# A decoder layer in fp32: the norms of the second queries and keys move from GpSimd to TensorE

## The chip, the cores and the metric

The kernel runs on one core of a Trainium2 chip. The metric is the device time of one launch in microseconds, the median of three runs. Profiles are of one execution taken by the hardware profiler; TensorE is called PE there, its weight loads PEld, VectorE DVE, ScalarE ACT, GpSimd POOL, and SyncE, which issues nearly all DMAs, SP.

## What is computed

A decoder layer on x (8 x 100 tokens of 1024) and a context (8 x 722 of 1024): a retention layer, an attention layer over context and own tokens, a gated feed-forward layer, each followed by a residual sum and a layer norm. The part that matters here stands at the start of the attention layer: queries (16 heads of 128) and keys (4 heads) are projected, each head is divided by the root of its mean square, and then turned by position (rope).

```python
def rms_norm(x, w, eps=EPS):
    var = jnp.mean(jnp.square(x), axis=-1, keepdims=True)
    return x * jax.lax.rsqrt(var + eps) * w
...
q = (x @ wq).reshape(B, L, NUM_HEADS, HEAD_DIM)
k = (x @ wk).reshape(B, L, NUM_KV_HEADS, HEAD_DIM)
v = (x @ wv).reshape(B, L, NUM_KV_HEADS, HEAD_DIM)
q = rms_norm(q, q_norm_w)
k = rms_norm(k, k_norm_w)
...
q = q * cos + rotate_half(q) * sin
k = k * cos + rotate_half(k) * sin
```

## The kernel before

Everything is fp32 in effect. An operand of a large matmul is split into a high and a low part in the reduced fp32 type (`split`, `split2`, lines 64 to 70: ScalarE casts the high part, VectorE subtracts for the low part), and `mm3` (lines 87 to 90) makes three passes of TensorE for one product. Small matmuls (sums over partitions, transposes, the first layer's scores) are plain fp32.

Features lie on partitions and tokens on the free axis. The 800 tokens are worked in two halves of N = 400 (4 sequences of 100). A "block" below is one projection of one head for one half: 128 features x 400 tokens, 24 passes (`proj`, lines 102 to 107), left in a PSUM bank. There are eight banks: three of tag a, four of tag s, one of tag v; projections take a and s in turn (`acc_tag`).

The stage in question is the loop at lines 608 to 640. For each of the four groups of heads it projects four queries, a key and a value (i = 0 to 3, 4, 5) in chunks of two weight matrices, or four in the first chunk, each chunk for both halves. Weights come in by SP (`load_w`, line 72, three raw buffers wst), and are split into one of four buffers w. A query or key block then goes through these steps:

1. line 631, ScalarE: squares sq out of the bank;
2. line 632, `all_red` (line 127), GpSimd: sum of the squares over the 128 partitions, on every partition;
3. line 634, `rope` (lines 135 to 139): two half copies on ScalarE, three products and sums on VectorE; the bank is free after line 137;
4. line 635, `inv_root` (lines 115 to 122): Ln, Exp, Square on ScalarE, two operations on VectorE, all on 128 x 400;
5. line 636, VectorE: the turned block times scale and root;
6. lines 639 and 640: split into d, one DMA to the DRAM tensor qd or kd.

A value block is transposed on TensorE (`tokens_first`, line 150) and written to vd. Into the same stage the context keys of the first two groups of heads are worked ahead (`context_keys`, lines 578 to 596), with four more GpSimd reductions at line 591 and weights from the DRAM tensor wcd (line 84). The loop over sequences from line 647 reads qd, kd and vd back. There, at lines 595 and 674, a row of sums already goes through DRAM to come back as a column.

The order of the instructions on each engine is not that of the text. The program is planned by a simulated timeline: at each step the planner gives an engine the earliest instruction of the text that is ready by its own estimates. On the chip each engine then runs its list in order and waits at semaphores, so a wait that is longer than planned holds all that stands behind it on that engine, DMA issues on SP included. Tiles of one tag share the buffers given by bufs, and a new tile waits for the last reader of the one before.

Of the kernel before, what the change touches and what calls it, by code (L numbers as in the profile page):

```python
# [8 lines left out]
F32 = mybir.dt.float32  # L9
FR = mybir.dt.float32r  # L10
AF = mybir.ActivationFunctionType
ALU = mybir.AluOpType
# [4 lines left out]
P = 128  # L17
B, T, D = 8, 100, 1024
NB = 4
N = NB * T  # L20
# [11 lines left out]
NKV = 4  # L32
# [9 lines left out]
def decoder_layer(ctx, tc, xT, cT, w1, wo1, w2, wo2, wc, w3, wd, gw, qw, kw, trig, dec, mask, out):  # L42
    nc = tc.nc

    def sbuf(name, bufs, side=None):
        return tc.tile_pool(name=name, bufs=bufs, side=side, reuse_waits="tile")
# [3 lines left out]
    dr = ctx.enter_context(tc.tile_pool(name="dr", bufs=1, space=DRAM))  # L50
# [4 lines left out]
    def bank(tag):  # L55
        return ps.tile([P, 512], F32, tag=tag, name=tag, bufs=banks[tag])

    def f32(ap):
        return ap.bitcast(F32)

    def bt(ap):
        return ap.rearrange("p (b t) -> p b t", b=NB)
# [5 lines left out]
    def split2(hi, lo, src):  # L68
        nc.scalar.copy(hi, src)  # L69
        nc.vector.tensor_tensor(lo, src, f32(hi), ALU.subtract)  # L70

    def load_w(src, w=None, parts=1):
        st = wp.tile([P, KT * P], F32, tag="wst", name="wst", bufs=3)
        if w is None:
            w = wp.tile([P, 2, KT * P], FR, tag="w", name="w", bufs=4)
        for i in range(parts):
            c = slice(i * KT * P // parts, (i + 1) * KT * P // parts)
            nc.sync.dma_start(out=st[:, c], in_=src[:, c])
            split(w[:, :, c], st[:, c])
        return w  # L80
# [17 lines left out]
    def acc_tag():  # L98
        turn[0] += 1
        return "as"[turn[0] % 2]  # L100

    def proj(w, z, n=N, tag="a"):
        acc = bank(tag)[:, :n]
        for k in range(KT):
            t = z[k // QT]
            mmw(acc, w, k, t[:, 0, k % QT, :n], t[:, 1, k % QT, :n], k == 0, k == KT - 1)
        return acc
# [1 line left out]
    def ln_exp():  # L109
        tc.keep_in_program_order(nc.scalar.preload_act_table_set(LN_EXP))  # L110

    def inv_root(pool, ss, eps, n=N, pin=False):

        r = pool.tile([P, n], F32, tag="r0", name="r0")
        ln = nc.scalar.activation(r, ss, AF.Ln, bias=eps)
        if pin:
            tc.keep_in_program_order(ln)
        nc.scalar.activation(r, r, AF.Exp, scale=-0.5)
        q = pool.tile([P, n], F32, tag="r1", name="r1")
        nc.scalar.activation(q, r, AF.Square)  # L120
        nc.vector.scalar_tensor_tensor(q, ss, eps, q, ALU.add, ALU.mult)  # L121
        nc.vector.scalar_tensor_tensor(q, q, 3.0, r, ALU.subtract, ALU.mult)  # L122
        return q

    def all_red(pool, x, tag, op=RED.add):
        y = pool.tile([P, N], F32, tag=tag, name=tag)
        nc.gpsimd.partition_all_reduce(y, x, P, op)  # L127
        return y

    def rope(pool, acc, cosw, sinw, tag="t1", op=ALU.add):  # L130

        t1 = pool.tile([P, N], F32, tag=tag, name=tag)
        t2 = pool.tile([P, N], F32, tag="t2", name="t2")
        h = P // 2
        nc.scalar.copy(t2[0:h], acc[h:P])
        nc.scalar.copy(t2[h:P], acc[0:h])
        nc.vector.tensor_tensor(bt(t1), bt(acc), cosw[:, None, :].to_broadcast([P, NB, T]), ALU.mult)
        nc.vector.tensor_tensor(bt(t2), bt(t2), sinw[:, None, :].to_broadcast([P, NB, T]), ALU.mult)
        nc.vector.tensor_tensor(t1, t1, t2, op)
        return t1  # L140
# [14 lines left out]
    qd = dr.tile([NKV, 4, P, B, 2, T], FR, name="qd")  # L155
    kd = dr.tile([NKV, P, B, 2, T], FR, name="kd")
# [20 lines left out]
    def const(v, name):  # L177
        t = cp.tile([P, 1], F32, name=name)
        nc.vector.memset(t, v)
        return t  # L180
# [3 lines left out]
    eps_k = const(128e-6, "eps_k")  # L184
# [219 lines left out]
    with sbuf("l1", 2) as p:  # L404
# [42 lines left out]
        qk, v, oo, ss = {}, {}, {}, {}  # L447
# [129 lines left out]

    def context_keys(kv):

        kall = ka.tile([P, 2, SC + T], FR, tag="kall", name="kall")  # L580
        wk = load_ws(2 * kv)
        sq = ka.tile([P, SC], F32, tag="ksq", name="ksq", bufs=1)
        ss = ka.tile([P, 6 * P], F32, tag="kss", name="kss", bufs=1)
        row = dr.tile([6, P], F32, tag="row", name="row", bufs=2)
        nc.gpsimd.memset(ss[:, SC:], 1.0)

        def step(hf):
            n, at = SN[hf], slice(hf * SH, hf * SH + SN[hf])
            acc = proj(wk, cz[hf], n)
            nc.scalar.activation(sq[:, at], acc, AF.Square)  # L590
            nc.gpsimd.partition_all_reduce(ss[:, at], sq[:, at], P, RED.add)  # L591
            nc.scalar.activation(kall[:, 0, at], acc, AF.Copy, scale=kws)
            nc.vector.scalar_tensor_tensor(kall[:, 1, at], acc, kws, f32(kall[:, 0, at]), ALU.mult, ALU.subtract)
            if hf:
                nc.sync.dma_start(out=row.rearrange("c p -> (c p)")[None, :], in_=ss[0:1])
        return step, (kall, row)
# [8 lines left out]
        return vt  # L605


    early = []
    with sbuf("l2", 2) as p:
        for kv in range(NKV):  # L610
            for i0, i1 in ((0, 4), (4, 6)) if kv == 0 else ((0, 2), (2, 4), (4, 6)):
                if (kv, i0) == (0, 4):
                    load_context(0)
                ws = [load_w(w2[kv, i]) for i in range(i0, i1)]
                if (kv, i0) in ((1, 2), (2, 2)):
                    step, kept = context_keys(kv - 1)
                    early.append(kept)
                if (kv, i0) in ((1, 2), (2, 0), (2, 2), (3, 0)):
                    step(i0 == 0)
                for half in range(2):  # L620
                    bs = slice(half * NB, (half + 1) * NB)
                    for i in range(i0, i1):
                        acc = proj(ws[i - i0], z1[half], tag=acc_tag())
                        if i == 5:
                            tr = tokens_first(p, acc).rearrange("p (b d) -> p b d", b=NB)
                            vs = p.tile([T, NB, 2, P], FR, tag="vs", name="vs", bufs=1)
                            split2(vs[:, :, 0], vs[:, :, 1], tr)
                            nc.sync.dma_start(out=f32(vd[kv, :, bs]), in_=f32(vs))
                            continue
                        sq = p.tile([P, N], F32, tag="sq", name="sq")  # L630
                        nc.scalar.activation(sq, acc, AF.Square)
                        ss = all_red(p, sq, "ss")
                        tb = tq if i < 4 else tk
                        t = rope(p, acc, tb[:, 0], tb[:, 1])
                        r = inv_root(p, ss, eps_k)
                        nc.vector.scalar_tensor_tensor(
                            t, t, -0.5 if i < 4 else -0.5 * math.sqrt(P), r, ALU.mult, ALU.mult)
                        d = p.tile([P, NB, 2, T], FR, tag="d", name="d", bufs=3)
                        split2(d[:, :, 0], d[:, :, 1], bt(t))
                        nc.sync.dma_start(out=f32(qd[kv, i, :, bs] if i < 4 else kd[kv, :, bs]), in_=f32(d))  # L640
    z1pool.__exit__(None, None, None)


# [2 lines left out]
    with sbuf("cx", 2) as p, sbuf("c1", 1) as p1:  # L646
        for b in range(B):
            if b > 0:
                load_context(b)
            for kv in range(NKV):  # L650
                if early:
                    kall, row = early.pop(0)
                else:
# [7 lines left out]
                q = p.tile([P, 4, 2, T], FR, tag="q", name="q")  # L661
                nc.sync.dma_start(out=f32(q).rearrange("p h l t -> p h (l t)"),
                                  in_=f32(qd[kv, :, :, b]).rearrange("h p l t -> p h (l t)"))
# [11 lines left out]
                r0 = p.tile([P, 6], F32, tag="rr0", name="rr0")  # L675
                nc.scalar.activation(r0, rr, AF.Ln, bias=eps_k)
                nc.scalar.activation(r0, r0, AF.Exp, scale=-0.5)
                r1 = p.tile([P, 6], F32, tag="rr1", name="rr1")
# [12 lines left out]
                for j, c in enumerate(ORDER):  # L691
                    rows, n, t0 = (R6, N6, T6) if c == 6 else (P, N, 0)
# [44 lines left out]
                r = p.tile([P, N], F32, bufs=1, tag="r0", name="r0")  # L737
# [4 lines left out]
                of = p.tile([P, N], F32, bufs=1, tag="ofs", name="ofs")  # L742
# [286 lines left out]
```

## Time and profile before

| | us |
|---|---|
| median of 3 runs | 2551.77 |
| lowest, highest | 2550.91, 2553.14 |
| the profiled execution | 2551.76 |
| its span, first to last instruction | 2550.0 |

The mean granted TensorE clock is 0.995. Groups of instructions between 600 and 860 us, which holds the stage (line, engine, operation, out<-in, shapes, count, then busy us and mean ns of one, then the engine's idle time before them and what ended it):

```profile
L127 POOL PARTITION_ALL_REDUCE ss<-sq x40 | 118.1, 2960 | 258.6 <-DMA zd<-y 166.6 <-ACT sq L631 38.6 <-DVE r L121 38.5
L122 DVE SCALAR_TENSOR_TENSOR r<-r,r 128x400 f32<-128x400 f32 x41 | 37.6, 917 | 0.3
L636 DVE SCALAR_TENSOR_TENSOR t<-t,r 128x400 f32<-128x400 f32 x40 | 32.1, 803 | 0.3
L138 DVE TENSOR_TENSOR t<-t,tq 128x400 f32<-128x400 f32 x32 | 31.2, 975 | 1.4 <-ACT t L136 1.4
L115 ACT ACTIVATE r<-ss,eps_k 128x400 f32<-128x400 f32 x40 | 25.1, 627 | 10.1 <-POOL ss L127 9.9
L118 ACT ACTIVATE r<-r 128x400 f32<-128x400 f32 x41 | 22.0, 537 | 0.5
```

A matmul's record runs until its result is in the bank, so records overlap: one of 400 columns takes 338 ns, while the next starts after 182 ns. The plain fp32 matmuls of line 307, on 400 columns, show as two records each.

### The profile page before, as it was taken

To read this page: it belongs to the slowest core of one execution; us is meant where nothing else is said; L and a number is where in the kernel's file an instruction comes from. 1 tells how busy PE (TensorE), PEld (TensorE's weight loads), DVE (VectorE), ACT (ScalarE), POOL (GpSimd) and SP (SyncE) were. 2 spreads that over 40 slices of the span, in tenths; PEclk is the share of its full clock that TensorE was granted. 3 is DMA by queue.
4 is the path that set the end of the run, shared out by engine and by line. 5 is a ranking of instruction groups with operands and counts; after the bars stand their busy time and mean duration, and the time that the engine had idled before them with its cause. 6 is when DMAs were issued, how large, how long until landed. Compare 5 with 4: busy or idle time off the path is not lost.

```text
span 2550.0 us, 37518 instructions
## 1 busy us (share of the span) xinstructions
PE 2504.3 (98%) x14186; PEld 2462.7 (97%) x14186; DVE 2006.9 (79%) x3316; ACT 1338.8 (53%) x2390; POOL 471.7 (18%) x230
## 2 busy tenths in 40 slices
PE   8999999998999999999999999999999999999997
PEld 8999999998899999999999999999999999999996
DVE  7778876569999788898998998767875865865886
ACT  6676676336777466565565565434432433432351
POOL 0111111002555243333343343100000000000000
PEclk9999999999999999999999999999999999999999
DMA  7333445764444555455455455474412211211221
GB/s 237 109 113 122 142 142 197 246 248 151 140 141 166 185 185 167 132 180 161 145 176 161 150 185 187 139 263 132 141 50 67 83 50 67 83 50 67 67 75 52
DMA packets 165940, 353.93 MB, mean 139 GB/s; under 512 B 45530, under 2 KB 108378, under 8 KB 156542
## 3 DMA queue, kind: packets, MB, share of 16 engines
q1 hardware_dynamic: 164606, 347.33, 40.9%
q0 software_dynamic: 1152, 4.19, 1.1%
q8 instruction: 111, 1.82, 0.3%
q14 instruction: 71, 0.58, 0.1%
HBM read 283.09 MB, written 68.39 MB: 138 GB/s over the span
## 4 chain that ended last, share of the span: by engine, by line
PE 87%; DVE 7%; DMA 2%; issue 2%; ACT 1%; SPq 0%; DVEq 0%; ACTq 0%
PE a L90 16%; PE a L88 16%; PE a L89 16%; PE s L89 10%; PE s L90 10%; PE s L88 10%; PE v L88 3%; PE v L90 2%; PE v L89 2%; DVE r L122 1%; PE s L473 1%; PE s L668 1%; DVE r L121 1%; DVE d L70 1%; DVE w L70 1%
## 5 line engine op out<-in xcount | busy, mean ns | idle before, releaser
L88 PE MATMUL a<-big,w 128*128 128x400 f32 (+2 forms) x1796 | 606.0, 338 | 9.7 <-ACT big L69 6.4
L89 PE MATMUL a<-big,w 128*128 128x400 f32 (+2 forms) x1796 | 606.1, 338 | 0.0
L90 PE MATMUL a<-big,w 128*128 128x400 f32 (+2 forms) x1796 | 604.3, 337 | 0.0
L69 ACT CAST w<-wst 128x1024 fp32r<-128x1024 f32 (+2 forms) x292 | 251.4, 864 | 260.4 <-PE a L90 112.0
L70 DVE TENSOR_TENSOR w<-wst,w 128x1024 fp32r<-128x1024 f32 (+2 forms) x292 | 290.7, 998 | 104.6 <-ACT w L69 103.3
L88 PEld LDWEIGHTS a<-big,w 128*128 128x128 f32 x1796 | 338.4, 188 | 10.9 <-ACT big L69 7.0
L89 PEld LDWEIGHTS a<-big,w 128*128 128x128 f32 x1796 | 338.7, 189 | 1.6 <-DVE big L70 0.6
L90 PEld LDWEIGHTS a<-big,w 128*128 128x128 f32 x1796 | 338.7, 189 | 0.7
L127 POOL PARTITION_ALL_REDUCE ss<-sq x56 | 161.2, 2885 | 332.7 <-DMA zd<-y 166.6
L88 PE MATMUL s<-big,w 128*128 128x400 f32 x596 | 207.9, 350 | 2.4 <-ACT big L69 2.4
L89 PE MATMUL s<-big,w 128*128 128x400 f32 x596 | 206.8, 347 | 1.7 <-DVE big L70 1.7
L90 PE MATMUL s<-big,w 128*128 128x400 f32 x596 | 206.3, 347 | 0.0
L591 POOL PARTITION_ALL_REDUCE kss<-ksq x64 | 165.5, 2586 | 140.8 <-ACT ksq L590 140.1
L69 ACT CAST w<-as 128x512 fp32r<-128x512 f32 x90 | 55.9, 621 | 214.2 <-PE a L90 180.1
L702 ACT ACTIVATE s<-s,rk 128x400 f32<-128x400 f32 x160 | 88.2, 592 | 95.1 <-DVE sm L724 64.5
L127 POOL PARTITION_ALL_REDUCE mb<-sm x32 | 83.4, 2607 | 217.5 <-DVE sm L724 217.5
L853 DVE TENSOR_TENSOR s<-s 128x400 f32<-128x400 f32 x183 | 102.3, 568 | 24.9 <-ACT s L849 19.2
L721 ACT ACTIVATE s<-s 128x800 f32<-128x800 f32 (+1 forms) x128 | 95.3, 749 | 45.6 <-DVE s L715 42.2
L88 PEld LDWEIGHTS s<-big,w 128*128 128x128 f32 x596 | 112.6, 189 | 4.5 <-ACT big L69 3.6
L89 PEld LDWEIGHTS s<-big,w 128*128 128x128 f32 x596 | 112.5, 189 | 3.2 <-DVE big L70 2.3
L90 PEld LDWEIGHTS s<-big,w 128*128 128x128 f32 x596 | 113.0, 190 | 0.0
L70 DVE TENSOR_TENSOR pl<-s,ph 128x800 fp32r<-128x800 f32 (+1 forms) x128 | 108.2, 850 | 1.1 <-ACT ph L69 1.0
(315 smaller groups left out, 6222.6 us busy)
## 6 DMA issues: line engine op xcount, KB each, us to landing
wst<-in_w SPq DMA_DIRECT2D x137, 512.0 KB
w<-wcd SPq DMA_DIRECT2D x64, 1024.0 KB
wst<-in_wo SPq DMA_DIRECT2D x64, 512.0 KB
wst<-in_wd SPq DMA_DIRECT2D x32, 512.0 KB
big<-o1d SPq DMA_DIRECT2D x16, 800.0 KB
qd<-d SPq DMA_DIRECT2D x32, 400.0 KB
q<-qd SPq DMA_DIRECT2D x32, 400.0 KB
o2d<-oh SPq DMA_DIRECT2D x32, 400.0 KB
```

The source lines that it names most:

```text
L69: nc.scalar.copy(hi, src)
L70: nc.vector.tensor_tensor(lo, src, f32(hi), ALU.subtract)
L88: nc.tensor.matmul(acc, lh, rh, start=start, stop=False, skip_group_check=chain)
L89: nc.tensor.matmul(acc, lh, rl, start=False, stop=False, skip_group_check=chain)
L90: nc.tensor.matmul(acc, ll, rh, start=False, stop=stop, skip_group_check=chain)
L121: nc.vector.scalar_tensor_tensor(q, ss, eps, q, ALU.add, ALU.mult)
L122: nc.vector.scalar_tensor_tensor(q, q, 3.0, r, ALU.subtract, ALU.mult)
L127: nc.gpsimd.partition_all_reduce(y, x, P, op)
L591: nc.gpsimd.partition_all_reduce(ss[:, at], sq[:, at], P, RED.add)
L702: nc.scalar.activation(sc, sp, AF.Copy, scale=rk[:, c:c + 1])
L721: nc.scalar.activation(e, e, AF.Exp)
L853: nc.vector.tensor_tensor(t, x, y, op)
```

## The change

The query and key blocks are no longer normed one by one. After the squares and the rope a block is put into a list; at four blocks `normed` works them together. Four matmuls with a matrix of ones, 128 x 32, each in its own 32 columns of the TensorE array (`tile_position`), leave the sums of block j on partitions 32j to 32j + 31 of the one bank of tag v. One root chain runs on these 128 partitions. One row of each quarter is written to a DRAM tensor rd, and for each block its row is read back onto all 128 partitions; then follow the product with the root, the split and the write as before. There are 40 such blocks, so ten groups; the last is complete after the second key block of the last group of heads. A group can span two groups of heads.

Buffers: sq from 2 to 6 (the rows that come back use the same six), the turned blocks t1 from 2 to 6, the root's r0 and r1 from 2 to 1, d from 3 to 2; ss has none left in SBUF. The row's root is read out of PSUM by ScalarE and VectorE.

```diff
-    def inv_root(pool, ss, eps, n=N, pin=False):
-
-        r = pool.tile([P, n], F32, tag="r0", name="r0")
+    def inv_root(pool, ss, eps, n=N, pin=False, parts=P, bufs=None):
+
+        r = pool.tile([P, n], F32, tag="r0", name="r0", bufs=bufs)[:parts]
...
-        q = pool.tile([P, n], F32, tag="r1", name="r1")
+        q = pool.tile([P, n], F32, tag="r1", name="r1", bufs=bufs)[:parts]
...
+        ones32 = p.tile([P, 32], F32, name="ones32", bufs=1)
+        nc.vector.memset(ones32, 1.0)
+
+        def normed(group):
+
+            ss = bank("v")[:, :N]
+            for j, (sq, _, _, _) in enumerate(group):
+                at = slice(32 * j, 32 * (j + 1))
+                nc.tensor.matmul(ss[at], ones32, sq, start=True, stop=True, tile_position=(0, 32 * j))
+            n = 32 * len(group)
+            r = inv_root(p, ss[:n], eps_k[:n], parts=n, bufs=1)
+            rd = dr.tile([4, N], F32, tag="rd", name="rd", bufs=2)
+            m = len(group)
+            with nc.allow_non_contiguous_dma("one row of each quarter"):
+                nc.sync.dma_start(out=rd[:m], in_=r.rearrange("(j r) n -> j r n", r=32)[:, 0])
+            for j, (_, t, scale, dst) in enumerate(group):
+                rb = p.tile([P, N], F32, tag="sq", name="rb", bufs=6)
+                nc.sync.dma_start(out=rb, in_=rd[j:j + 1].partition_broadcast(P))
+                nc.vector.scalar_tensor_tensor(t, t, scale, rb, ALU.mult, ALU.mult)
+                d = p.tile([P, NB, 2, T], FR, tag="d", name="d", bufs=2)
+                split2(d[:, :, 0], d[:, :, 1], bt(t))
+                nc.sync.dma_start(out=f32(dst), in_=f32(d))
...
-                        sq = p.tile([P, N], F32, tag="sq", name="sq")
+                        sq = p.tile([P, N], F32, tag="sq", name="sq", bufs=6)
                         nc.scalar.activation(sq, acc, AF.Square)
-                        ss = all_red(p, sq, "ss")
                         tb = tq if i < 4 else tk
-                        t = rope(p, acc, tb[:, 0], tb[:, 1])
-                        r = inv_root(p, ss, eps_k)
-                        nc.vector.scalar_tensor_tensor(
-                            t, t, -0.5 if i < 4 else -0.5 * math.sqrt(P), r, ALU.mult, ALU.mult)
-                        d = p.tile([P, NB, 2, T], FR, tag="d", name="d", bufs=3)
-                        split2(d[:, :, 0], d[:, :, 1], bt(t))
-                        nc.sync.dma_start(out=f32(qd[kv, i, :, bs] if i < 4 else kd[kv, :, bs]), in_=f32(d))
+                        t = rope(p, acc, tb[:, 0], tb[:, 1], bufs=6)
+                        group.append((sq, t, -0.5 if i < 4 else -0.5 * math.sqrt(P),
+                                      qd[kv, i, :, bs] if i < 4 else kd[kv, :, bs]))
+                        if len(group) == 4 or kv == NKV - 1 and i == 4 and half == 1:
+                            normed(group)
+                            group.clear()
```

More of the change, by code (lines that the diff above doesn't have):

```diff
@@ L128, in all_red, with rope @@
         return y
-    def rope(pool, acc, cosw, sinw, tag="t1", op=ALU.add):
-        t1 = pool.tile([P, N], F32, tag=tag, name=tag)
+    def rope(pool, acc, cosw, sinw, tag="t1", op=ALU.add, bufs=None):
+        t1 = pool.tile([P, N], F32, tag=tag, name=tag, bufs=bufs)
         t2 = pool.tile([P, N], F32, tag="t2", name="t2")
@@ L605, in context_values @@
         return vt
-    early = []
+    early, group = [], []
     with sbuf("l2", 2) as p:
+        ones32 = p.tile([P, 32], F32, name="ones32", bufs=1)
[18 more added lines that the diff above has]
+                nc.sync.dma_start(out=f32(dst), in_=f32(d))
         for kv in range(NKV):
```

## The prediction, made before the changed kernel was run

> **What bounds the kernel now.** I read the page first: TensorE is busy for 98% of the span, so a change is worth what it does to TensorE's own stream. The stage that the change touches (the second layer's projections, lines 608 to 640) runs from about 596 to 842 us. I cut it into stretches by busy time, at the places where the granted clock changes. Columns: stretch, its length, then busy us and instruction count of PE, PEld, DVE, ACT, POOL; granted clock, DMA share, GB/s.
>
> ```profile
> span 2550.0 us, 37518 instructions
> PE 2504.3 (98%) x14186; PEld 2462.7 (97%) x14186; DVE 2006.9 (79%) x3316; ACT 1338.8 (53%) x2390; POOL 471.7 (18%) x230
> ...
> 607.60:611.00 3.40, 3.40 (x11) 3.40 (x12) 3.40 (x8) 2.71 (x6) 3.05 (x1) 0.50 0.50 183
> 611.00:634.90 23.90, 19.58 (x109) 19.27 (x107) 23.23 (x29) 18.15 (x33) 13.88 (x6) 1.00 0.33 103
> 634.90:638.30 3.40, 3.40 (x10) 3.40 (x11) 3.40 (x5) 0.77 (x2) 2.22 (x2) 0.50 0.48 191
> 638.30:699.70 61.40, 56.17 (x311) 55.03 (x310) 59.84 (x87) 42.57 (x86) 36.72 (x12) 1.00 0.42 141
> 699.70:706.60 6.90, 5.87 (x17) 5.29 (x18) 6.87 (x9) 5.74 (x11) 4.22 (x2) 0.51 0.29 87
> 706.60:842.00 135.40, 132.97 (x744) 131.60 (x743) 125.39 (x180) 95.35 (x184) 69.65 (x27) 1.00 0.47 157
> ```
>
> The reader is to see that VectorE is full (97% or more) up to 706 us, that TensorE has holes there and runs at half clock for 3.4 and 6.9 us after two of them, and that after 706 us TensorE is full itself (132.97 of 135.40). The waits of TensorE in this stage, 600 to 860 us (waiter, releaser, us in total, times, longest):
>
> ```profile
> PE a L88 <- ACT r L120: 4.3, 1, 4.3
> PE a L88 <- ACT w L69: 3.1, 1, 3.1
> PE s L150 <- ACT vt L147: 3.0, 4, 0.9
> PE a L88 <- DMA w<-wcd: 2.2, 1, 2.2
> PE s L89 <- DVE z L70: 2.0, 1, 2.0
> PE s L668 <- ACT cvt L604: 0.6, 1, 0.6
> PE a L90 <- DVE w L70: 0.3, 1, 0.3
> ```
>
> The first is ascribed to L120, but the order of time shows what it was: the bank comes free with VectorE's L137, which ends at 634.74, and TensorE starts at 634.88. VectorE was late because of this:
>
> ```profile
> 628.69 2.86 POOL L127 PARTITION_ALL_REDUCE ss<-sq  x1 [1.83 <-DVE r L121]
> 629.01 2.11 DVE L122 SCALAR_TENSOR_TENSOR r<-r,r 128x400 f32<-128x400 f32 x1
> ...
> 634.18 0.56 DVE L137 TENSOR_TENSOR t<-a,tq 128x400 f32<-128x400 f32 x1
> 634.35 2.60 POOL L127 PARTITION_ALL_REDUCE ss<-sq  x1 [2.79 <-DVE r L121]
> 634.66 1.85 DVE L122 SCALAR_TENSOR_TENSOR r<-r,r 128x400 f32<-128x400 f32 x1
> ```
>
> An operation of 0.56 us takes 1.85 to 2.11 us when GpSimd starts a reduction beside it. The second wait (weight split L69 on ScalarE) is the same backlog one engine further: that split stood behind a cast which waited 3.71 us for VectorE's L636.
>
> **What the Trainium skill says.** "GPSIMD Engine Reference", Key points: GpSimd shares its SBUF interfaces with VectorE, and instructions with two SBUF inputs contend. The trace agrees (L122, two SBUF inputs: 0.56 alone, up to 2.11). "TensorE: Matmul & The Clock Gate", Part 1: after an idle window of some 3.4 us the clock falls to half. The trace agrees: 0.50 for 3.4 us after the 4.3 us gap. The same page, Part 3: column tiles run side by side, matmuls keep program order, and three column tiles of 512 columns gave 2.38 times the speed. "TensorEngine Tiling (Array Packing)", Key Properties: changing the tiling mode drains TensorE. No row of before uses column tiles, so the last two are not shown by it.
>
> **The change part by part.** Forty blocks (4 groups of heads x 5 x 2 halves) are normed, ten groups of four.
>
> *Removed from GpSimd:* 40 of the L127 reductions, 118.1 us busy between 600 and 860 us. Only the four of L591 stay in this stage. GpSimd is bound by nothing here; what goes is the contention. VectorE's mean for L122 is 917 ns against 0.56 undisturbed, for L138 on queries 975, for L636 803: 0.35 x 40 + 0.41 x 32 + 0.24 x 40 = 37 us, and L139, the casts' low parts and the weights bring it to about 50 us.
>
> *Removed from VectorE and ScalarE:* 30 of 40 root chains. VectorE: 60 x 0.56 = 34 us. ScalarE: L115, L118, L120 at 627, 537, 537 ns: 30 x 1.70 = 51 us. VectorE falls from some 237 us in 264 to about 155, ScalarE from 177 to 126. Against TensorE's 4.4 us for a block (24 passes of 0.182 us) neither is a bound any more.
>
> *What that gives TensorE:* the gap at 634.88 lost 4.5 us, and the half clock behind it 1.7 (half of 3.4). The gap at 700.45 lost 3.3, two small ones behind it 1.0, the half clock 3.3. The transpose at 641.73 waited 0.7. Sum 14.5. Of the 2.2 us for w<-wcd (its issue stood on SP behind a kd write that waited for VectorE) I count half, of the other transposes' waits of 2.3 us half: 2.3 together. The hole at 607 (2.0 and half clock) belongs to the layer before and stays. Gain: 17 us, at most 20, at least 12 if a hole survives.
>
> *Added on TensorE:* 40 fp32 matmuls of 128x32 on 400 columns. The nearest row is L307/L300, fp32 with 128 columns of weights: in order of time L300's first starts at 593.36 and L307's at 594.03, so 0.67 us each, in two halves of 0.33 (two records a matmul). One after another: 10 x 4 x 0.67 = 26.7 us. All four abreast: 10 x 0.67 = 6.7. In between, and my choice: since matmuls keep order and the second half of a tile needs that same tile again, only the second half of one tile can lie beside the first half of the next: five slots of 0.33, 1.67 us a group, 16.7 in all. The drain on entering and leaving the tiled mode isn't in the trace; a matmul's record is 338 ns where the next starts after 182, so its tail is about 0.16; one such tail a group is an estimate, 1.5 us; ends 0 and 3. TensorE is full here, so nothing hides this.
>
> *Added wait on TensorE:* the group's matmuls stand in its queue until ScalarE has squared the last block; all later projections are behind them. The nearest row is the transposes behind ScalarE's copy: 3.0 us in 4 of 8 cases, 0.4 each. With ScalarE half idle I take 0.2 each, 2 us; ends 0 and 5.
>
> *Added DMAs on SP:* per group one row write, four broadcasts of 200 KB, and the same four writes of d as before, now in a bunch with 2 buffers in place of 3. SP's broadcasts wait there for the row to land, and weight loads stand behind. The nearest pair is row<-kss and rr<-row: SP waited 2.0 us a time for the row (46.8 in 23), and ScalarE waited for rr 13.9 us in 32 (12 waits, up to 6.1). So a hop costs 2 to 3 us, two about 5, and the planned order mostly allows for it. VectorE's L636 successor and ScalarE's split wait on it, with copies out of PSUM behind them. Cover: seven banks, of which projections can run some five ahead (22 us), and slack of 40% on VectorE. I take nothing; without cover 10 groups x 0.5 to 2 us. The 8 MB added over 250 us are 32 GB/s beside 160, hidden.
>
> *The end of the stage:* the last kd write was issued at 852.35, 13.1 us after its square at 839.23, since ScalarE stood 6 us at vs. The new chain (0.5 square, 1.9 matmuls, 1.7 + 1.1 root, two hops 5, four times 0.6 of VectorE) is about 13 too, and TensorE has context keys and values to do meanwhile (full from 842 on, but for 0.6). Nothing.
>
> Sum: -17 + 16.7 + 1.5 + 2 = +3. The profiled execution took 2551.76 us (span 2550.0, 1.8 around it), the median of the runs is 2551.77, so both give 2555.
>
> **The rivals.**
> A, the forecast: five slots, backlog gone: 2555, own range 2549 to 2560. Chance 0.36.
> B, the four tiles abreast (the page's 2.38 for three speaks for it, the two halves of an fp32 matmul against): 6.7 + 1.5 + 1 - 17 = -8: 2544, range 2540 to 2549. Chance 0.34.
> C, no overlap at all: 26.7 + 1.5 + 2 - 17 = +13: 2565. Speaks for it: no tiled row here; against: the page. Chance 0.13.
> D, slower by another way: the DRAM hops. The broadcasts land behind weight loads of 512 KB, VectorE and ScalarE stand in order at the group's first product and at the two d buffers, the next group's square is late and TensorE waits at the summing matmuls. vd<-vs, issued at 839.70, held ScalarE until 846.71; were two hops 4 us longer than planned and a quarter of that not covered, 10 groups cost 10 us: 2565. It decides from 1 us a group. Chance 0.13.
> E, the gain is larger (all 20 us, and abreast): 2540. Chance 0.04.
>
> **How the numbers follow.** A measurement of this kernel can tell about 0.2%, 5.1 us, from no change: the bounds are 2546.7 and 2556.9. Faster: 0.02 of A, 0.28 of B, E: 0.34. Same: 0.24 of A, 0.06 of B, 0.02 of C and D: 0.32. Slower: 0.10 of A, 0.24 of C and D: 0.34. Range 2542 to 2567; it takes in most of B, all of A, and C and D up to a little beyond their centres.
>
> **What would show it.** Right: VectorE's share between 611 and 706 us falls below 75%, no half clock after 611, L122 ten times in the stage at 0.56 us. The step of summing: start of a group's first to the next projection's matmul, 1.7 to 2.0 us (A), 0.7 to 1.0 (B), 2.7 to 3.0 (C). D would show as waits of ScalarE's d or VectorE's t for the broadcast, and of TensorE for sq. I am wrong if TensorE still has holes above 1 us after 611, or if the stages after 860 us change by more than 2 us.

## The result and the profile after

The changed kernel takes 2584.74 us (median of 4 runs, 2583.29 to 2585.84) where the kernel before took 2552.26 in the same session: a ratio of 1.0127, 95% interval 1.011 to 1.0145. That is 32.5 us slower. The forecast of 2555 and its range up to 2567 are both missed.

The first view is the head of the page of the kernel after (span, then busy time of each engine), the second its windows over the stage and the time up to the first scores. Columns of the second are as before: stretch, length, busy us and count of PE, PEld, DVE, ACT, POOL; granted clock, DMA share, GB/s.

```profile
span 2584.1 us, 37590 instructions
...
PE 2534.0 (98%) x14266; PEld 2465.5 (95%) x14266; DVE 1943.4 (75%) x3257; ACT 1293.5 (50%) x2300; POOL 358.1 (14%) x190
```

```profile
610.90:706.00 95.10, 95.10 (x489) 82.20 (x487) 58.42 (x100) 51.68 (x95) 2.45 (x1) 1.00 0.45 158
706.00:852.40 146.40, 146.01 (x781) 131.86 (x780) 84.44 (x144) 70.16 (x131) 8.44 (x5) 1.00 0.51 177
852.40:880.60 28.20, 26.01 (x161) 25.62 (x159) 7.99 (x16) 6.37 (x15) 4.83 (x2) 1.00 0.78 273
880.60:887.40 6.80, 4.45 (x15) 4.46 (x16) 2.18 (x9) 1.94 (x6) 0.14 (x1) 0.50 0.45 98
```

The reader is to see two things. From 611 to 852 us TensorE has no hole left and runs at full clock; VectorE is busy for 58.42 of 95.10 us (61%), where it was at 97% or more before. Behind 852 us there is something new: TensorE is idle for 2.2 us in one stretch and 2.35 in the next, and at half clock for 6.8. The two largest waits of TensorE from 600 to 887 us (waiter, releaser, us in total, times, longest) name it:

```profile
PE s L88 <- DMA q<-qd: 4.5, 1, 4.5
PE s L89 <- DVE z L70: 2.5, 1, 2.5
```

The first scores of the sequence loop wait for the first queries out of DRAM. The second line is the hole of the layer before, at 607 us, which was there already.

To account for the 32.5 us I took three landmarks from the start times of TensorE's instructions: the last projection of the stage, the first score matmul behind it, and the first matmul of each sequence of the loop. All are us from the span's start. The profiled execution of the kernel after took 2585.84 us, 34.1 more than that of the kernel before, so the landmarks add up to a little more than 32.5. The first three differences are running totals; the last is what the six later sequences add.

| | before | after | difference |
|---|---|---|---|
| last projection of the stage | 838.6 | 848.2 | +9.6 |
| first score matmul | 860.5 | 883.0 | +22.5 |
| second sequence begins | 944.3 | 969.2 | +24.9 |
| each later sequence | 96.6, six times | 99.7, 99.7, 98.5, 98.3, 96.6, 96.6 | +9.7 in all |

So only 9.6 us are lost in the stage that the prediction summed up. The rest arises behind it, in code that the change doesn't touch.

**In the stage.** Counted as what the steps from pass to pass exceed 0.182 us by, holes and half clock lost about 23 us of the kernel before here; some 5 of these are left, so about 18 came back. The summing matmuls took it all and 9.6 more. This is the timeline of PE at one of them (start, duration, engine, line, operation; the two records of an fp32 matmul are one line, x2):

```profile
616.47 0.34 PE L88 MATMUL s<-z,w 128*128 128x400 f32 x1
616.74 0.86 PE L619 MATMUL v<-sq,ones 128*32 128x400 f32 x2
617.53 0.46 PE L89 MATMUL s<-z,w 128*128 128x400 f32 x1
617.83 0.34 PE L90 MATMUL s<-z,w 128*128 128x400 f32 x1
```

It stands alone between projections. The next one follows at 618.83: the planner put each sum into TensorE's list by itself, 1.5 to 12.5 us behind the end of its own square, and did not keep the four of a group together. The 40 stand in 29 places. From the start of the projection ahead to that of the second one behind are 1.36 us (616.47 to 617.83); two passes of 0.182 taken off, the place costs 0.99. It costs that whether it holds one, two or three of them, and the 29 places add up to 28.5 us, of which 27.5 lie ahead of the last projection.

**The hand-over.** The last group of blocks is complete late, and the sequence loop waits for its writes. SP's own timeline (issues of DMAs), and below it that of ScalarE and VectorE:

```profile
855.54 0.51 SPq L625 DMA_DIRECT2D rd<-r  x1
857.93 0.33 SPq L84 DMA_DIRECT2D w<-wcd  x1
859.49 1.75 SPq L628 DMA_DIRECT2D rb<-rd  x4
...
871.41 1.64 SPq L632 DMA_DIRECT2D kd<-d  x2
...
875.52 0.39 SPq L684 DMA_DIRECT2D q<-qd  x1
```

```profile
847.28 0.51 ACT L655 ACTIVATE sq<-s 128x400 f32<-128x400 f32 x1 [3.36 <-PE s L90]
...
865.70 1.61 DVE L629 SCALAR_TENSOR_TENSOR t<-t,rb 128x400 f32<-128x400 f32 x3 [7.23 <-DMA rb<-rd]
...
870.25 0.53 ACT L69 CAST d<-t 128x400 fp32r<-128x400 f32 x1 [2.87 <-DMA qd<-d]
```

From the last square (847.28) to the issue of the last of kd's writes (872.74, the second of the two at 871.41) are 25.5 us, where the kernel before needed 13.1 (839.23 to 852.35). From the row's issue to the first issue of its way back are 3.9 us (855.54 to 859.49), with a weight load issued in between; VectorE gets the row 6.2 us later (865.70). Then four blocks go through two buffers d: the third split stood until the first write had left its buffer.

**Behind it.** Before, TensorE waited for nothing between the first scores and 1600 us. After, from 887 to 1640 us, the largest wait is this:

```profile
PE a L88 <- DVE kall L593: 8.4, 5, 2.1
```

Four of the five, of 1.6 to 2.1 us, come one in each of the first four sequences, for the context keys of the next one. The timeline of the first of these four:

```profile
941.66 1.01 ACT L592 ACTIVATE kall<-a,kws 128x362 fp32r<-128x362 f32 x2
943.67 1.09 DVE L593 SCALAR_TENSOR_TENSOR kall<-a,kws,kall 128x362 fp32r<-128x362 f32 x2
944.32 0.43 PE L88 MATMUL a<-big,w 128*128 128x360 f32 x1 [1.98 <-DVE kall L593]
```

The two halves' splits now stand as a pair behind other work in the lists of ScalarE and VectorE, and so both banks come free at once. The order in which ScalarE ran them shows it: before, square (L590) and split (L592) of the two halves come as square, split, square, split in all 32 units (one unit is a group of heads of one sequence); after, they come as square, square, split, split in 11 of the 15 units from the third to the seventeenth, which belong to the first four sequences and the beginning of the fifth. From the eighteenth unit on the old order is back, and from the sixth sequence on so are the 96.6 us. Two of the waits cost more than themselves: behind them, from 945.4 and from 1245.8 us, TensorE runs at half clock for 3.4 us.

### The profile page after: what moved, and what is told of

It reads as the page before. It is cut to its first block, busy times and chain, and to the rows that moved or that the text cites. A ratio compares the mean times of both kernels' runs of the same rounds, so it can differ in the third digit from the quotient of the medians.

```text
span 2584.1 us, 37590 instructions
## 1 busy us (share of the span) xinstructions
PE 2534.0 (98%) x14266; PEld 2465.5 (95%) x14266; DVE 1943.4 (75%) x3257; ACT 1293.5 (50%) x2300; POOL 358.1 (14%) x190
## 4 chain that ended last, share of the span: by engine, by line
PE 87%; DVE 5%; DMA 3%; ACT 2%; issue 1%; SPq 0%; POOL 0%; DVEq 0%; ACTq 0%
PE a L88 16%; PE a L90 16%; PE a L89 16%; PE s L89 10%; PE s L88 10%; PE s L90 10%; PE v L88 2%; PE v L90 2%; PE v L89 2%; PE s L473 1%; DMA wst<-in_w 1%; PE v L619 1%; DVE big L70 1%; DMA cs<-in_cT 1%; PE s L690 1%
## 5 line engine op out<-in xcount | busy, mean ns | idle before, releaser
L591 POOL PARTITION_ALL_REDUCE kss<-ksq x64 | 169.5, 2649 | 630.0 <-ACT ksq L590 629.6
L875 DVE TENSOR_TENSOR s<-s 128x400 f32<-128x400 f32 x183 | 102.4, 569 | 24.6 <-ACT s L871 19.6
L725 DVE TENSOR_TENSOR mx<-mx,s 128x400 f32<-128x400 f32 x128 | 82.1, 641 | 19.5 <-ACT s L724 15.8
```

The lines of the kernel that those rows point to most:

```text
L725: nc.vector.tensor_tensor(mx, s[:, 1] if j == 2 else mx, sc, ALU.max)
L875: nc.vector.tensor_tensor(t, x, y, op)
```

## The experiments

My theories, as the first two views left them: the sums cost what the prediction had not priced, by standing apart; the late hand-over costs the rest. The rival to the second was that the order of the next stage, which the planner chooses anew in every version, is a cost of its own.

**e1: the four sums side by side.** The last block's sum is issued first (it is ready last), the other three only behind it.

```diff
-            for j, (sq, _, _, _) in enumerate(group):
-                at = slice(32 * j, 32 * (j + 1))
-                nc.tensor.matmul(ss[at], ones32, sq, start=True, stop=True, tile_position=(0, 32 * j))
+            def summed(j):
+                at = slice(32 * j, 32 * (j + 1))
+                return nc.tensor.matmul(ss[at], ones32, group[j][0], start=True, stop=True, tile_position=(0, 32 * j))
+            last = summed(len(group) - 1)
+            with tc.issue_after(last.ins):
+                for j in range(len(group) - 1):
+                    summed(j)
```

> The changed kernel with the four summing matmuls of a group put next to each other in TensorE's list (the last block's first, the other three queued behind it); all else as in the changed kernel. In the changed kernel the planner placed each of the four as soon as its own square was ready, 80 records lying singly among the projections, and they cost 25.6 us. Theory 'singly placed, so one after another': adjacent they share the array. Five slots of 0.33 us a group: 17 us in all, time 2576; all four abreast: 7 to 9 us, time 2567 or so. Rival 'column tiles of plain fp32 don't overlap at all': 27 us as now, time 2585.

2582.16 us, ratio 1.0116 [1.0101, 1.0131]. PE's timeline at one group:

```profile
617.14 0.35 PE L88 MATMUL a<-z,w 128*128 128x400 f32 x1
617.42 0.88 PE L619 MATMUL v<-sq,ones 128*32 128x400 f32 x8
618.23 0.45 PE L89 MATMUL a<-z,w 128*128 128x400 f32 x1
618.51 0.35 PE L90 MATMUL a<-z,w 128*128 128x400 f32 x1
```

Eight records, four whole matmuls, cost 1.01 us (617.14 to 618.51 less two passes): the price of one alone. Record by record the four first halves start within 0.02 us, at 617.42 to 617.44, and the four second halves 0.36 later. Ten groups cost 10.7 us, where the 29 places of the kernel after cost 28.5 (the expectation had 25.6), and the stage ends at 829.2, 9.3 us earlier than in the kernel before. Yet the whole is only 2.6 us better than the changed kernel: behind the stage the first scores come 36.2 us later (865.4) instead of 21.9, and the sequences take 98.7 to 102.4.

**e2: the last four blocks in the old way** (each on GpSimd, with its own chain), so that the end of the stage has no DRAM hop.

```diff
...
+                        count += 1
+                        if count > 36:
+                            alone(*block)
+                            continue
```

> The changed kernel with its last group (four blocks) normed one by one on GpSimd as before; nine groups as in the changed kernel. Theory 'late hand-over': the 24 us lost after the last projection come from the last group's chain (25.4 us from the last square to the last kd write, 13.1 before) and go almost wholly: 2560 to 2564, first scores of the next stage some 12 to 13 us earlier against the last projection. Rival 'the next stage is slower for another reason' (other buffers, the bank of tag v, freed GpSimd): 2580 to 2586.

2564.95 us, 1.0052 [1.0037, 1.0067]: 19.8 us better than the change. The chain from the last square to the last write is 10.9 us, the first scores come at 868.7. But this gain is not the hand-over's alone: from the fourth sequence on, the loop runs in 96.6 us as before.

**e3: only the last four blocks in the new way.** The reverse of e2.

```diff
...
+                        if count <= 36:
+                            alone(*block)
+                            continue
```

> The reverse of the kernel with the last group alone: blocks 1 to 36 normed one by one on GpSimd, and only the last four as the change does it (singly placed matmuls on column tiles, one root chain, rows by way of DRAM); some buffers fewer than before (sq 4, t1 5, ss 1, d 2). Theory 'late hand-over': the stage itself as before, then 20 to 25 us lost after it: 2572 to 2580. Rival 'the change's first nine groups leave the planner another order': 2550 to 2558.

2619.28 us, 1.027 [1.0255, 1.0285]. It tells nothing of the hand-over: to make room for both ways I had to give sq four buffers, the turned blocks five and ss one, and the stage stalled by itself: TensorE waited for L137 to free a bank 5 times, 29.8 us in all.

**e4 and e5: sums on TensorE without column tiles.** The kernel before, with each block's squares summed by a 128x128 matrix of ones into the bank of tag v, and its own root chain; in the reduced fp32 type (e4) and in plain fp32 (e5). This prices a sum by itself.

```diff
...
-                        ss = all_red(p, sq, "ss")
+                        ss = bank("v")[:, :N]
+                        nc.tensor.matmul(ss, oner, sq, start=True, stop=True)
```

> The kernel before, with one change: each block's squares are written in the reduced fp32 type and summed on TensorE by one pass with a 128x128 matrix of ones, into the bank of tag v, on all partitions; root chain block by block, no trip through DRAM. The squares lose low bits. Theory: TensorE pays 40 x 0.18 = 7 us and gains the 15 us of holes and half clock, and the hand-over is as early as before: 2542 to 2546. Rival 'the wait for the square in TensorE's queue costs most': 40 waits of 0.4 to 1 us, 2560 or more. Rival 'VectorE is still full with 40 root chains': holes stay, 2555.

> As the kernel with squares in the reduced type, but squares and ones in plain fp32: four times the TensorE time for the sums and nothing else. Theory: 40 x 0.67 = 27 us against 7: 20 us above that kernel, 2562 to 2566, holes gone, hand-over early. If the sums were not on the bound, the two would be equal. Rival 'waits for the squares rule': both far above 2570.

e4 2614.93 us, 1.0244 [1.0229, 1.026]; e5 2629.43, 1.0298 [1.0281, 1.0315]. Both are far over what I had expected. The single bank of tag v held TensorE up until VectorE had read it; e4's wait:

```profile
PE v L637 <- DVE r L121: 26.4, 7, 4.6
```

The difference of the two is clean of that only in part: 14.5 us for 40 plain sums in place of 40 reduced ones. The traces price a sum better. PE's timeline at one of e5's:

```profile
647.13 0.35 PE L88 MATMUL s<-z,w 128*128 128x400 f32 x1
647.32 0.83 PE L635 MATMUL v<-sq,one 128*128 128x400 f32 x2
647.68 0.65 PE L89 MATMUL s<-z,w 128*128 128x400 f32 x1
648.17 0.34 PE L90 MATMUL s<-z,w 128*128 128x400 f32 x1
```

Counted as above (647.13 to 648.17 less two passes) an untiled fp32 sum costs 0.67 us, where a column-tiled one that stands alone costs 0.99. Forty untiled ones would take 26.8 us, less than the 28.5 of the change: in 29 places the tiles save nothing.

**e6: e1 and e2 together**, sums side by side and the last four in the old way (the edits of both).

> Both edits at once: the summing matmuls adjacent, and the last group normed one by one. With adjacency alone the projections ended 9.4 us earlier than in the kernel before, though the time was 2582; with the last group alone the next stage came back to within 5 us of before. Theory 'two separate faults': they add, 2552.6 - 9.4 + 0 to 6: 2543 to 2549, faster than before. Rival 'the next stage's order is a matter of chance, not of the hand-over': 2560 to 2585.

2578.73 us, 1.0111 [1.0096, 1.0126]. This is the run that felled my theory of the hand-over. The stage ends at 831.5 and the first scores come at 855.2, 5.3 us earlier than in the kernel before; and the kernel is 27 us slower than the kernel before all the same. The sequences take 99.7 to 102, and TensorE's wait between 600 and 1700 us is the one for the context keys:

```profile
PE a L88 <- DVE kall L593: 15.8, 11, 2.1
```

**e8: the last group's rows spread by TensorE.** Sums side by side; in the last group a row is put on all partitions by a matmul with a column of the identity, without DRAM.

```diff
...
+                    rb = bank("s")[:, :N]
+                    nc.tensor.matmul(rb, ident[:, 32 * j:32 * j + 1].to_broadcast([P, P]), r, start=True, stop=True)
...
```

> Adjacent matmuls; the last group is still normed together, but its four rows are spread over the partitions by four fp32 matmuls with a column of the identity (0.67 us each) instead of going through DRAM. If the two DRAM hops (3.9 and 6.2 us in the changed kernel's last group) make the hand-over late: as with the last group alone, 2543 to 2552, last square to last kd write 14 us or less. If the bunch of four splits and writes through two d buffers does: still 20 us lost after the stage, 2560 to 2575.

2583.52 us, 1.012 [1.0104, 1.0136]. The chain from square to last write is 19.0 us, against 25.9 in e1 and 10.9 in e6: of the 15 us between the new end and the old one, the two DRAM hops are 7; the rest is put down here to the bunching of the four blocks, which no run separates. The total does not move, since the sequences again take 98.5 to 100.7 each.

**e7: e4 with the sums in two tags of banks.** Each block's sum takes a bank of tag s or v in turn, so that no single bank holds TensorE up. No column tile, no group, no DRAM hop.

```diff
...
-                        ss = bank("v")[:, :N]
+                        ss = bank({"a": "s", "s": "v"}[tag])[:, :N]
```

> The kernel that sums squares in the reduced type block by block (low bits of the squares dropped), with its sums in the banks of tags s and v in turn instead of v alone. There TensorE waited 26.4 us, 7 times, for the one bank to be read by L121. Theory 'the single bank was the fault': those waits go and the 60 us with them, 2544 to 2556. Rival 'the wait for each square and each root chain in strict order': above 2580.

2580.04 us, 1.0107 [1.009, 1.0123]. The most telling run of the first half: its last projection is at 838.5, its first scores at 860.1, its second sequence begins at 944.3, each within 0.5 us of the kernel before, where e4's last projection was at 882.9; the single bank was the fault there. Then the sequences take 100.3, 103.7, 101.2, 100.8, 99.7 and 101.0. These six lose 27 us in a stage whose instructions are the same and whose start is the same.

That left the order. The part from the sequence loop on has 7090 instructions in every one of these kernels, the same set. Set against the kernel before, e6's list for TensorE has them at places 12.5 apart on average (up to 61), ScalarE's 2.8, VectorE's 3.0.

**e9 to e12: the pair of the context keys held.** The square of the second half is kept behind the split of the first in ScalarE's list, in the kernel after (e9), in e1 (e10), in e6 (e11), and in the kernel before as a control (e12).

```diff
...
+            if hf:
+                tc.add_manual_dep(square.ins, first[0].ins.name, mybir.DependencyInfo(
+                    mybir.DependencyClass.NoSync, mybir.DependencyReason.DATA), reason="order")
```

> The changed kernel with one order pinned in the next stage: in context_keys the second half's square (L590) may stand in ScalarE's list only behind the first half's copy (L592). Read from the lists: the kernel before has square, copy, square, copy in all 32 key units; in the changed kernel the planner put square, square, copy, copy in units of sequences 0 to 3, and just these sequences took 98 to 100 us in place of 96.6, with TensorE waiting some 2 us for L593 in each. Theory 'another planned order, not the late hand-over, makes the later loss': sequences 1 to 4 at 96.6 us, some 9 to 12 us less: 2572 to 2577. Rival 'the pattern goes along with the loss but doesn't make it': 2580 to 2586, waits for L593 or another one stay.

> Adjacent summing matmuls, all ten groups as in the change, and the same pinned order. Without the pin all sequences took 99 to 102 us here (2582 in all). Theory: 96.6 us from sequence 1 on, 20 to 25 us less: 2556 to 2563; what is left over the kernel with the last group alone is the price of the late hand-over. Rival as above: 2578 to 2584.

> Adjacent matmuls, last group alone, pinned order. The first scores of the next stage came at 855.2 us without the pin, 5.3 earlier than in the kernel before; with 96.6 us for a sequence that stays: 2545 to 2550, faster than before. Rival: the planner finds another bad order, 2560 or more.

> Control: the kernel before with the pinned order alone. Its list has that order in all units already, so nothing should change: 2550 to 2554, every sequence at 96.6 us.

e9 2591.02 us, 1.0151 [1.0136, 1.0166]; e10 2573.15, 1.0081 [1.0064, 1.0098]; e11 2561.2, 1.0034 [1.0021, 1.0047]; e12 2551.7, 1.0 [0.9992, 1.0009]. The control costs nothing, two of the three get better by 9 and 17.5 us, but the kernel after gets worse by 6, and in all three the sequences still take 97.8 to 101.2, though the pattern is gone from all their units. It is not the cause by itself.

**e13 to e16: the whole order held.** From the sequence loop on, each engine's instructions are put in the order that they have in the kernel before, by a dependency from each to the one ahead of it that orders the list and waits for nothing; the stage of the change is left to the planner. Of the kernel after (e14), of e1 (e15), of e6 (e13), of e7 (e16).

```diff
+    begun = len(nc.cur_bb.bb.instructions)
     ...
+    in_order(tc, nc.cur_bb.bb.instructions[begun:])
```

> The changed kernel, with all instructions of the next stage (scores, softmax, context keys and values; 7090 of them) held in the order, engine by engine, that the planner gave them in the kernel before; the changed stage in front is planned freely. Theory 'the planned order of the next stage makes the later loss': sequences 1 to 7 take 96.6 us, and what is left is the 9.7 us of the projections and the late hand-over, 0 to 8 us: 2562 to 2570. Rival 'the loss hangs on something that stays when the order is that of before (addresses, the late hand-over itself)': sequences at 98 to 100 us, 2580 or more.

> Adjacent summing matmuls, all ten groups, and the next stage in the order of the kernel before. Theory 'order': projections 9.4 us shorter than before, sequences at 96.6 us, late hand-over 0 to 8: 2543 to 2551. Rival: 2565 or more as with the one pinned pair (2573).

> Adjacent summing matmuls, last group alone, the next stage in the order of the kernel before. Theory 'order': first scores about 5 us earlier than before, sequences at 96.6 us: 2545 to 2549. Rival: 2560 or more as with the one pinned pair (2561).

> Squares in the reduced type (low bits dropped), summed block by block by one pass of TensorE into two banks, the next stage in the order of the kernel before. Without that order this kernel reached the first scores at 860.1 and sequence 1 at 944.3 us, to 0.4 us as the kernel before, and then took 100 to 104 us for a sequence in place of 96.6 (2580 in all). Theory 'order': 2550 to 2554. Rival: 2575 or more.

| edit | order planned anew | order of before | the order alone |
|---|---|---|---|
| the change (e14) | 2584.74 | 2568.92, 1.0067 [1.0052, 1.0082] | 15.8 |
| sums side by side (e1, e15) | 2582.16 | 2552.31, 1.0001 [0.9993, 1.001] | 29.9 |
| and last four as before (e6, e13) | 2578.73 | 2544.96, 0.9973 [0.9963, 0.9983] | 33.8 |
| no tiles, no groups (e7, e16) | 2580.04 | 2550.46, 0.9993 [0.9985, 1.0002] | 29.6 |

The two columns are from different sessions, between which the kernel before moved by less than 1 us (2551.8 to 2552.6); e15 lies 1.3 us above what was expected, the other three within it or at its edge. In the traces of all four, TensorE, ScalarE and VectorE run the loop from the second sequence on in the very order of the kernel before, and every sequence from there on takes 96.6 us. One of them, in the kernel after and in e14 (windows, columns as above):

```profile
969.20:1068.90 99.70, 97.06 (x576) 94.17 (x575) 88.96 (x151) 58.25 (x113) 36.73 (x20) 1.00 0.46 148
```

```profile
963.70:1060.30 96.60, 96.60 (x577) 94.52 (x576) 86.56 (x152) 58.01 (x113) 37.16 (x21) 1.00 0.50 162
```

TensorE's busy time is the same but for 0.5 us; the 2.6 us of idle time are gone. e14's largest wait from 600 to 1640 us is again that for the first queries, 7.3 us. Of the 15.8 us that the order gives back there, 4.3 come ahead of the first scores (878.6 in e14, 883.0 in the kernel after), so not all of the late start was the hand-over's. With the order settled, the runs can be set against each other part by part; the stage itself is still planned anew, and its last projection moves by up to 1.5 us. The texts of e15 and e13 differ in the last four blocks alone: 7.4 us for the late hand-over, with the tenth group's sums in it. The kernel after is then 9.6 (stage) + 7.4 (hand-over) + 15.8 (order) = 32.8, where 32.5 were measured. The three terms are from different runs, so the fit to 0.3 us is in part luck; e14 itself stands 16.9 above the kernel before, where the first two terms make 17.0.

e13 is faster than both kernels: 2544.96 us (9 runs, 2543.1 to 2547.32) against 2552.07 for the kernel before.

## Why the prediction was wrong, and where it was right

**Right: the bound, and what its removal gives.** "Gain: 17 us, at most 20, at least 12" was about 18. VectorE fell to 61% (below 75% was the sign given), there is no half clock in the stage after 611 us, and the operations that suffered beside GpSimd run at their own speed. Groups of the kernel after, 600 to 900 us (line, engine, operation, out<-in, count | busy, mean ns of one | idle ahead of it and what ended it):

```profile
L69 ACT CAST d<-t 128x400 fp32r<-128x400 f32 x40 | 21.1, 528 | 44.8 <-DVE t L629 21.4 <-DMA qd<-d 16.7 <-DVE t L137 2.4
L629 DVE SCALAR_TENSOR_TENSOR t<-t,rb 128x400 f32<-128x400 f32 x40 | 22.3, 572 | 38.6 <-DMA rb<-rd 38.3
...
L138 DVE TENSOR_TENSOR t<-t,tq 128x400 f32<-128x400 f32 x32 | 19.4, 605 | 0.0
L121 DVE SCALAR_TENSOR_TENSOR r<-v,eps_k,r 128x400 f32<-128x400 f32 x10 | 6.3, 633 | 17.5 <-ACT r L120 17.4
```

L138 is at 605 ns where it took 975, the product with the root at 572 where it took 803; there are ten root chains. L122, named at 0.56 us, takes 0.57 to 0.58 in nine of its ten places; in the tenth, at 722.37, it takes 1.73: it began 0.26 us after one of the reductions that stay (L591, 722.11).

**Right: the cover of the DRAM hops within the stage.** The same lines show VectorE waiting 38.3 us for rows and ScalarE 16.7 for buffers d. TensorE did not notice it before 852 us: "I take nothing" held for nine groups of ten, and rival D, which wanted it at each group, is out.

**Right, and smaller: the wait for the squares.** 2 us were taken; TensorE's weight loads for the sums waited 0.3 us for a square and 0.5 for a half copy. This is in part luck, since each sum stood some way behind its own square; in e1, where the sums wait for the last one, the matmuls waited 0.7 us once.

**Wrong: "five slots of 0.33, 1.67 us a group, 16.7 in all" with 1.5 for the drain.** Measured: 28.5. Two things failed in this step. The first is the premise that the four stand together. The text of the change has them in one loop, but the order is the planner's, and the section on the kernel before says that it takes what is ready first; I applied that to waits and not to the sums. Ten groups became 29 places. The second is the mechanism. I held that the second half of a tile must follow its first before the next tile's second can start, which gave five slots; e1 shows four first halves at once and then four second halves, so the tiles do lie abreast, as the Trainium skill has it ("TensorE: Matmul & The Clock Gate", Part 3). The step that the prediction named as its sign is 0.81 us in e1 (617.42 to 618.23), in rival B's band. A group of four is two halves of 0.33 and about 0.34 on top, 1.0 us in all. The untiled sums of e5, at 0.67 us a place, do not pay the 0.34, so it comes with the tiles; that it is the drain of "TensorEngine Tiling (Array Packing)", Key Properties, fits but is not shown apart from the narrower weights. Rival B had the right overlap, for e1 and not for the change: it forecast -8 us, and e13, which has the sums side by side and neither of the other two losses, measures -7.1. That is in part luck, as nine groups of sums cost 10.3 us there where B had 8.2 for ten. Rival C's 26.7 us for the sums lay near the 28.5 of the change for a wrong reason: two or three sums in one place cost no more than one, so they do overlap.

**Wrong: "The end of the stage ... is about 13 too ... Nothing".** The chain took 25.5 us and cost 7.4. Two hops were put at 5 us and took 10.2 in this group (855.54 to 865.70, with a weight load of 1 MB issued between them); the root chain began 4.8 us behind the start of the last square (852.03), where 2.4 were taken for square and sums; and four blocks through two buffers d took 7.0 from the first product to the last write, where four times 0.6 stood. Most of it was hidden behind the context keys and values, as stated, but not all.

**Missing: the order of the next stage.** No term of the sum had it, though the last sentence of the prediction named the stages behind 860 us as a place where it would fail. The planner's list for the sequence loop depends on its estimates for all that goes before; another text in one stage gives another list in the next. It is 15.8 us of the 32.5 here, and 29.6 to 33.8 in three other versions. Even e7, which reaches the loop within 0.5 us of the kernel before, has it. That the order does it is shown by e13 to e16. Why the planner's estimate prefers the slower order, and which of the moved instructions is the one that counts, is not shown: holding the one pair that I could name gave back 9.0 and 17.5 us in two versions, cost 6.3 in the third, and brought no sequence to 96.6 us (e9 to e11).

The first theory on the way, that a late hand-over makes all the loss behind the stage, was wrong as well: e6 hands over earlier than the kernel before and is still slow.

## What to carry to other kernels

Where a planner orders the instructions, price a change with the order that it will give, not that of the text: ask of each added instruction whether anything keeps it beside its companions, and look at stages that the edit leaves alone, for their order may change too. Before judging an edit by its time, hold the order of the untouched part fixed and measure again; here the same idea is 1.3% slower or 0.3% faster, by the order and two details. Column tiles pay only if their matmuls are neighbours, and a chain that closes a stage should be the short one, even if the long one is right for all the others.

## What the runs showed of the hardware

- A column-tiled fp32 matmul of 128x32 on 400 columns costs 0.99 us alone between untiled passes, and four of them together 1.01, against 0.67 for one untiled fp32 matmul (e5; also from the start of one to that of the next, 593.36 to 594.03 in the kernel before).
- The two halves of four tiled fp32 matmuls are interleaved: four first halves within 0.02 us, 0.36 us later the four second halves.
- Writing a row to DRAM and reading it back onto 128 partitions took 10.2 us from the first issue to the first use, with a load of 1 MB issued between; the nearest pair of the kernel before had suggested about 5.
- How much GpSimd's reductions slow VectorE depended on when an operation began, as far as GpSimd's times in a profile can be trusted. In the kernel before, ten of the 40 L122 of the stage took 1.85 to 2.11 us; all ten began 0.15 to 0.43 us after a reduction's start. Of the other 30, at 0.55 to 0.58 us, one began in that span (0.24); those that were already running when a reduction began, or began 0.7 us or more into one, were not slowed. L138 and L636 were slowed later in a reduction too. L137, which reads one input from a PSUM bank, took 0.56 to 0.58 us in all 40 cases, ten of them begun 0.18 to 0.95 us into a reduction.
- TensorE's clock was set anew on a grid of 3.413 us: the half-clock stretches of the kernel after begin at 607.50, 880.57, 945.42 and 1245.79, that is 80, 19 and 88 steps apart. Over all 18 traces, a step at full clock with 1.9 us or more of idle TensorE in it, counted from the records (101 steps), was always followed by half clock, one with 1.2 to 1.55 us (78 steps) never; between these it went either way. The idle window of some 3.4 us, with which the prediction explained the half clock, does not fit this, and the measurement decides: 1.98 us of idle ahead of 945.42 were enough, while the 2.15 us from 1043.79 lay across a border of the grid (1044.41) and had no half clock behind them.
